# Normalized tokens stored from ScalarE's queue, and a reordered opening, in a linear-attention and mixture-of-experts kernel

## The chip, the cores and the metric

The kernel runs on one core of a Trainium2 chip. The metric is device time in microseconds (us) of one execution, lower is better. The core has five engines with a queue each: TensorE (PE, matrix products into PSUM), VectorE (DVE), ScalarE (ACT), GpSimd (POOL), and SyncE (SP), which issues transfers. ScalarE and GpSimd issue transfers too. [...]

## The reference

The input is 4 batches of 1,024 tokens of 256 channels, so 4,096 tokens. All is float32.

```
xn = layernorm(x)                       # no scale, no offset, eps 1e-5
y  = x + attention(xn) + ffn(xn)
attention: q, k, v = xn @ w_q.T, ...    # 16 heads of 16 channels, elu(.)+1 on q and k
           local  = causal linear attention, state carried from chunk to chunk of 128 tokens
           memory = the same queries read against 4 stored memories, coarse and fine, mixed by a gate
           output = (g * memory + (1-g) * local) @ w_o.T
ffn:       logits = xn @ gate_weight.T; the two best of 8 experts for each token
           each expert and one shared expert: silu(xn @ wg.T) * (xn @ wu.T) @ wd.T
```

What matters for the change is the first line: each token's 256 channels get a mean and a variance, and the normalized token feeds everything else.

## The kernel before, in words

**Tiling.** Tokens are taken in 8 blocks of 512, each held as 4 tiles of 128 tokens (partitions) by 256 channels. Block `b` lives in one SBUF tile called `x_b`. That tile serves twice: first it holds the input tokens, normalized in place, and then the same bytes are overwritten by the values `v` of the block (line 367, with small fills from GpSimd on lines 372 and 373). So the values of a block can be written only when every reader of its normalized tokens has finished.

**Readers of a normalized block.** There are two. TensorE transposes it (line 344), and a transfer stores it to the DRAM tensor `xns` (line 335), from which the expert stage later gathers rows by index (line 990).

**The opening stage.** It has four steps for each block, and the string `ahead` (line 1185) gives their order over blocks by hand:

- `S`, `statistics`: on VectorE, a `bn_stats` and a `bn_aggr` for each of the 4 tiles (lines 303, 304), then, once for block 0, once for each pair of blocks 1 and 2, 3 and 4, 5 and 6, and once for block 7, an add on VectorE and a power on GpSimd that makes `rstd` (lines 309, 312).
- `N`, `normalize`: `shift` on VectorE (319), tiles 2 and 3 on VectorE (326), tiles 0 and 1 on ScalarE (331), then the store to `xns` on SP's queue (335).
- `T`, `transpose_x`: for each of two pairs of tiles, four transposes on TensorE (344) and one copy to `xnT` on ScalarE (347).
- `V`, `values`: for each pair, the product with `w_vg` on TensorE (362), then ScalarE copies `v` into `x_b` (367) and the expert logits into `lgs` (371), and GpSimd fills the gaps (372, 373). Its PSUM pool `ps_v` has two buffers, one for each pair in flight.

The other words of `ahead` are small set-up steps: `masks` and `memories` on VectorE, `gates` on VectorE and ScalarE, `living` on TensorE and VectorE, and `route` on VectorE, which picks experts for the first half of the tokens.

**Transfers ahead of it.** SP's queue carries the 8 loads of `x` (512 KB each), then the memories and small vectors, then `w_o` and the shared expert's weights (lines 121 to 144), then the 8 stores to `xns`, then 8 copies of 512 KB from `x` to the DRAM tensor `sums` (line 1209, DRAM to DRAM, needed when the experts add their results), and two fills from a zero tile (1210, 1211). ScalarE's queue carries `w_vg`, `w_q` and `w_k`.

**After the opening.** Projections of queries and keys, a sort of the tokens by expert, then 32 rounds of attention mixed with 71 expert tiles, and a tail that adds the parts. These follow hand-weighted lists that the change leaves alone.

Of the kernel before, what the change touches and what calls it, by code (L numbers as in the profile page):

```python
# [11 lines left out]
ALU = mybir.AluOpType  # L12
AX = mybir.AxisListType

P = 128
NT = 4
TB = P * NT
EPS = 1e-6
LN_EPS = 1e-5
# [3 lines left out]
def linear_attention_moe_kernel(  # L23
# [28 lines left out]
    nc = tc.nc  # L52
# [17 lines left out]
    NBLK = T // TB  # L70
# [29 lines left out]
    def load_x(blk):  # L100

        wide = big.tile([P, NT, VW], FP, tag="tok", name=f"x_{blk}")
        xb = wide[:, :, :H]
        nc.sync.dma_start(
            xb, x[blk * TB : (blk + 1) * TB, :].rearrange("(n p) h -> p n h", p=P)
        )
        st["x", blk] = xb
        st["wide", blk] = wide

    for blk in range(NBLK):  # L110
        load_x(blk)

    def load_weight(w, name, engine=nc.sync):
        t = const.tile([P, NC, w.shape[1]], FP, tag=name, name=name)
        engine.dma_start(t, w.rearrange("(k p) c -> p k c", p=P))
        return t

    wvg = load_weight(w_vg, "wvg", nc.scalar)
    wq = load_weight(w_q, "wq", nc.scalar)
    wk = load_weight(w_k, "wk", nc.scalar)  # L120
    raw = const.tile([P, NC, NMN, D1], FP, tag="raw", name="raw")
    nc.sync.dma_start(
        raw[:, :, 1:NMN, :], memories.rearrange("(c p) m k -> p c m k", p=P)
# [33 lines left out]
    neghalf = const.tile([P, 2 * NT], FP, tag="neghalf", name="neghalf")  # L157
# [70 lines left out]
    gates = const.tile([P, H], FP, tag="gates", name="gates")  # L228
# [61 lines left out]
        nc.vector.tensor_scalar(alive, tot[:, :NMN], EPS, None, ALU.is_ge)  # L290


    def statistics(blk):

        xb = st["x", blk]
        if blk == 0 or blk % 2:
            st["mv"] = small.tile([P, 2, NT, 2], FP, tag="mv", name=f"mv_{blk}", bufs=3)
            st["rstd"] = small.tile([P, 2, NT], FP, tag="rstd", name=f"rstd_{blk}", bufs=3)
        mv, rstd = st["mv"], st["rstd"]
        at = (blk + 1) % 2 if blk else 0  # L300
        for i in range(NT):
            stats = small.tile([P, 6], FP, tag="stats", name=f"stats_{blk}_{i}")
            nc.vector.bn_stats(stats, xb[:, i, :])
            nc.vector.bn_aggr(mv[:, at, i, :], stats)
        st["norm", blk] = mv[:, at], rstd[:, at]
        if blk % 2 == 0 or blk == NBLK - 1:
            n = at + 1
            some = rstd[:, :n].rearrange("p b i -> p (b i)")
            nc.vector.tensor_scalar(
                some, mv[:, :n, :, 1].rearrange("p b i -> p (b i)"), LN_EPS, None, ALU.add  # L310
            )
            nc.gpsimd.tensor_tensor(some, some, neghalf[:, : n * NT], ALU.pow)

    def normalize(blk):

        xb = st["x", blk]
        mv, rstd = st.pop(("norm", blk))
        shift = small.tile([P, NT], FP, tag="shift", name=f"shift_{blk}")
        nc.vector.scalar_tensor_tensor(
            shift, mv[:, :, 0], -1.0, rstd, ALU.mult, ALU.mult  # L320
        )
        xnT = io.tile([P, NC, TB], FP, tag="xnT", name=f"xnT_{blk}")
        st["xnT", blk] = xnT
        half = NT // 2
        for i in range(half, NT):
            nc.vector.tensor_scalar(
                xb[:, i, :], xb[:, i, :], mv[:, i, 0:1], rstd[:, i : i + 1],
                ALU.subtract, ALU.mult,
            )
        for i in range(half):  # L330
            nc.scalar.activation(
                xb[:, i, :], xb[:, i, :], AF.Identity,
                bias=shift[:, i : i + 1], scale=rstd[:, i : i + 1],
            )
        nc.sync.dma_start(
            xns[blk * TB : (blk + 1) * TB, :].rearrange("(n p) h -> p n h", p=P), xb
        )

# [843 lines left out]
        return runs  # L1182


    ahead = "S0 S1 masks N0 T0 S2 S3 N1 N2 V0 T1 T2 S4 memories V1 S5 N3 N4 V2 T3 T4 S6 gates V3 S7"
    ahead += " N5 N6 V4 living T5 T6 N7 V5 route V6 T7 V7"
    other = {
        "masks": masks, "memories": memories_by_group, "gates": gates_of_heads, "living": living,
        "route": lambda: [None for _ in route(0)],
# [1 line left out]
    with tc.tile_pool(name="ps_v", bufs=2, space=bass.MemoryType.PSUM) as ps_v:  # L1191
        for what in ahead.split():
            if what in other:
                other[what]()
                continue
            blk = int(what[1:])
            if what[0] == "S":
                statistics(blk)
            elif what[0] == "N":
                normalize(blk)  # L1200
            else:
                for pair in range(NT // 2):
                    (transpose_x if what[0] == "T" else values)(blk, pair)
# [3 lines left out]
    for blk in range(NBLK):  # L1207
        rows = slice(blk * TB, (blk + 1) * TB)
# [110 lines left out]
```

## Time and profile before

| what | value |
|---|---|
| median of 3 runs | 736.98 us (736.46 to 739.15) |
| the profiled execution's own time | 731.18 us |
| its span, first to last instruction | 729.5 us |
| busy: PE, DVE, POOL, ACT | 653.1, 455.9, 386.0, 266.8 us |
| PE busy in the first 60.1 us | 40.78 us |
| PE busy from 60 to 90 us | 29.8 us |
| PE busy from 300 to 600 us | 294.5 us |

The span is cut into a start (to 60.1 us, all eight blocks normalized, transposed and projected to values), a dense middle, and a tail. In lines from the timeline the first number is the start in us, the second the time that the group took, then engine, line, operation, output and input, and in brackets the engine's idle time before it with what ended it. A line of the list of waits reads: engine and line that waited, whom it waited for, us in total, number of waits, longest.

### The profile page before, as it was taken

How to read it: one execution, taken by the hardware profiler on the slowest of the kernel's cores; microseconds unless marked ns; L12 is line 12 of the kernel's file. 1: busy time of each engine (PE TensorE's matmuls, PEld its weight loads, DVE VectorE, ACT ScalarE, POOL GpSimd, SP SyncE). 2: the span in 40 equal slices, each digit the busy share in tenths (PEclk: the TensorE clock that was granted, in tenths of full speed). 3: DMA queues.
4: the chain of work that ended last, by engine and by line, in shares of the span. 5: the costliest groups of instructions: out<-in, count | busy, mean ns of one | idle time of the engine just before them, and what ended most of it. 6: DMA issues, size and time to landing. Idle time of an engine off the chain costs nothing. (4 is left out here: it accounts for less than half of the span.)

```text
span 729.5 us, 14268 instructions
## 1 busy us (share of the span) xinstructions
PE 653.1 (90%) x5084; PEld 465.3 (64%) x5084; DVE 455.9 (62%) x1193; ACT 266.8 (37%) x614; POOL 386.0 (53%) x436
## 2 busy tenths in 40 slices
PE   3599986879999999999999999999999998997295
PEld 3485465756676776766676767666776665676274
DVE  6444888984656665665666646656666556667262
ACT  3365443423433443334433443344332433333010
POOL 3210034553656675655566666466664656666464
PEclk9799989999999999999999999999999999999598
DMA  9456000013444564454444544454554545552563
GB/s 292 156 198 190 0 1 1 2 52 89 106 116 99 123 127 96 104 119 106 116 116 107 128 109 120 93 129 101 122 126 96 134 112 108 130 127 40 153 200 123
DMA packets 86563, 81.51 MB, mean 112 GB/s; under 512 B 7629, under 2 KB 84093, under 8 KB 86365
## 3 DMA queue, kind: packets, MB, share of 16 engines
q1 hardware_dynamic: 67629, 57.00, 27.3%
q0 software_dynamic: 13632, 18.62, 15.5%
q10 hardware_dynamic: 5232, 4.99, 2.0%
q8 instruction: 40, 0.66, 0.4%
q14 instruction: 30, 0.25, 0.1%
HBM read 62.62 MB, written 22.15 MB: 116 GB/s over the span
## 5 line engine op out<-in xcount | busy, mean ns | idle before, releaser
L1058 POOL DMA_INDIRECT sums<-y,islot x71 | 113.4, 1597 | 70.6 <-DMA sums<-y,islot 15.1
L1042 DVE SCALAR_TENSOR_TENSOR hidden<-hidden,phe 128x176 f32<-128x176 f32 x71 | 23.8, 335 | 122.4 <-ACT hidden L1041 122.4
L1036 PE MATMUL phe<-wgu,turned 128*128 128x352 f32 x276 | 96.9, 474 | 2.5 <-ACT turned L1029 2.1
L698 DVE TENSOR_TENSOR sT<-quad,causal 128x512 f32<-128x512 f32 x128 | 80.4, 681 | 8.3 <-PE quad L691 7.8
L828 POOL TENSOR_TENSOR cg<-coarse,gates 128x256 f32<-128x256 f32 x32 | 24.3, 760 | 109.3 <-DVE h L883 61.1
L990 POOL DMA_INDIRECT xg<-xns,islot x71 | 70.6, 994 | 17.7 <-issue 9.7
L1049 PE MATMUL pye<-wdn,turned 88*128 88x256 f32 x284 | 75.5, 388 | 4.2 <-PE pu L786 3.0
L1036 PEld LDWEIGHTS phe<-wgu,turned 128*128 128x128 f32 x276 | 48.5, 191 | 26.2 <-issue 6.4
L1049 PEld LDWEIGHTS pye<-wdn,turned 88*128 88x128 f32 x284 | 50.1, 189 | 20.1 <-issue 8.5
L1053 ACT ACTIVATE y<-pye,wslot 128x256 f32<-128x256 f32 x71 | 33.6, 473 | 70.6 <-PE pye L1049 70.3
L846 POOL TENSOR_TENSOR fm<-fm 128x512 f32<-128x512 f32 x32 | 41.7, 1304 | 26.2 <-DVE prob L892 13.1
L1041 ACT ACTIVATE hidden<-phe 128x176 f32<-128x176 f32 x71 | 22.6, 318 | 86.7 <-PE phe L1036 79.7
L1029 ACT COPY turned<-pte 128x512 f32<-128x512 f32 (+1 forms) x71 | 41.2, 580 | 35.6 <-PE pte L1027 34.6
L953 PE MATMUL po<-wd,h 128*128 128x256 f32 (+1 forms) x192 | 49.5, 395 | 0.8 <-ACT oc L868 0.7
L905 PE MATMUL pg<-xnT,wg 128*128 128x512 f32 (+1 forms) x96 | 48.2, 627 | 0.0
L919 PE MATMUL psu<-xnT,wu 128*128 128x512 f32 (+1 forms) x96 | 46.1, 603 | 0.5 <-DVE loc L751 0.5
L835 DVE TENSOR_TENSOR fm<-quad,rw 128x512 f32<-128x512 f32 x64 | 42.2, 680 | 0.0
L953 PEld LDWEIGHTS po<-wd,h 128*128 128x128 f32 (+1 forms) x192 | 35.8, 196 | 7.7 <-ACT oc L868 1.2
L362 PE MATMUL pv<-wvg,xnT 128*128 128x264 f32 x128 | 33.1, 420 | 8.2 <-ACT xnT L347 8.2
L560 POOL TENSOR_TENSOR held<-ones,two 128x213 f32<-128x213 f32 (+1 forms) x22 | 16.0, 737 | 44.5 <-DVE ones L540 44.5
L806 PE MATMUL quad<-mem,sqT 32*128 32x170 f32 x512 | 27.6, 328 | 9.1 <-DVE sT L698 9.1
L894 DVE SCALAR_TENSOR_TENSOR o<-diff,prob,loc 128x256 f32<-128x256 f32 x32 | 33.1, 1035 | 3.4
(210 smaller groups left out, 1374.5 us busy)
## 6 DMA issues: line engine op xcount, KB each, us to landing
wgu<-in_w_gate_dram SPq DMA_DIRECT2D x71, 176.0 KB
wgu<-in_w_up_dram SPq DMA_DIRECT2D x71, 176.0 KB
wdn<-in_w_down_dram SPq DMA_DIRECT2D x71, 176.0 KB
x<-in_x_dram SPq DMA_DIRECT2D x8, 512.0 KB
xns<-x SPq DMA_DIRECT2D x8, 512.0 KB
sums<-in_x_dram SPq DMA_DIRECT2D x8, 512.0 KB
part<-sums SPq DMA_DIRECT2D x12, 256.0 KB
out_dram<-acc ACTq DMA_DIRECT2D x12, 256.0 KB
```

Of the source, the lines that this page charges most:

```text
L698: nc.vector.tensor_mul(sT, quad[:, g, :].rearrange("p (c t) -> p c t", t=P), causal[:, None, :].to_broadcast([P, NC * 2, P]),)
L835: nc.vector.tensor_mul(fm[:, c].rearrange("p g m (r k) -> p g (m r) k", k=HD), quad[:, :, c * KM + KX + KN : (c + 1) * KM].rearrange("p g ...
L846: nc.gpsimd.tensor_add(fm[:, :, 0:2, :], fm[:, :, 0:2, :], fm[:, :, 2:4, :])
L905: nc.tensor.matmul(pg[:n, :], wg[:, k, f * P : f * P + n], xnT[:, k, :], start=(k == 0), stop=(k == NC - 1),)
L919: nc.tensor.matmul(pu[:n, :], wu[:, k, f * P : f * P + n], xnT[:, k, :], start=(k == 0), stop=(k == NC - 1),)
L953: nc.tensor.matmul(po[:, :H], st["h", blk, f][:k, tok], wd[:k, f, :], start=(f == 0), stop=False)
L990: nc.gpsimd.indirect_dma_start(out=xg, out_offset=None, in_=xns, in_offset=bass.IndirectOffsetOnAxis(ap=islot[:, j : j + 1], axis=0),)
L1029: nc.scalar.copy(dst[:, lo:hi], pt[:, lo:hi])
L1036: nc.tensor.matmul(ph[:, : 2 * F], xgT[:, k, :], wgu[:, k].rearrange("p g f -> p (g f)"), start=(k == 0), stop=(k == NC - 1),)
L1049: nc.tensor.matmul(py[:, :H], hT[:FH, f, :], wdn[:, f, :], start=(f == 0), stop=(f == 1))
L1053: nc.scalar.activation(y, py[:, :H], AF.Copy, scale=wslot[:, j : j + 1])
L1058: nc.gpsimd.indirect_dma_start(out=sums, out_offset=bass.IndirectOffsetOnAxis(ap=islot[:, j : j + 1], axis=0), in_=st.pop(("y", j)), in_of ...
```

## The change

There are four edits. The tokens of block 0 are loaded in two parts of 256 KB, the second from ScalarE's queue. `w_q` and `w_k` move from ScalarE's queue to SP's, behind the tokens. The stores to `xns` move from SP's queue to ScalarE's. And `statistics` can do half a block, with a new order of the steps: block 1's statistics come in two halves around the normalization of block 0, and each block's transposes (`T`) come just before its own values, with the statistics, normalizations and set-up steps placed differently among them.

```diff
-        nc.sync.dma_start(
-            xb, x[blk * TB : (blk + 1) * TB, :].rearrange("(n p) h -> p n h", p=P)
-        )
+        parts = 2 if blk == 0 else 1
+        n = NT // parts
+        for part in range(parts):
+            rows = slice((blk * NT + part * n) * P, (blk * NT + (part + 1) * n) * P)
+            (nc.scalar if part else nc.sync).dma_start(
+                xb[:, part * n : (part + 1) * n],
+                x[rows, :].rearrange("(n p) h -> p n h", p=P),
+            )
...
     wvg = load_weight(w_vg, "wvg", nc.scalar)
-    wq = load_weight(w_q, "wq", nc.scalar)
-    wk = load_weight(w_k, "wk", nc.scalar)
+    wq = load_weight(w_q, "wq")
+    wk = load_weight(w_k, "wk")
...
-    def statistics(blk):
+    def statistics(blk, some=slice(0, NT)):
...
-        if blk == 0 or blk % 2:
+        if some.start == 0 and (blk == 0 or blk % 2):
...
-        for i in range(NT):
+        for i in range(some.start, some.stop):
...
-        if blk % 2 == 0 or blk == NBLK - 1:
+        if some.stop == NT and (blk % 2 == 0 or blk == NBLK - 1):
...
-        nc.sync.dma_start(
+        nc.scalar.dma_start(
             xns[blk * TB : (blk + 1) * TB, :].rearrange("(n p) h -> p n h", p=P), xb
         )
...
-    ahead = "S0 S1 masks N0 T0 S2 S3 N1 N2 V0 T1 T2 S4 memories V1 S5 N3 N4 V2 T3 T4 S6 gates V3 S7"
-    ahead += " N5 N6 V4 living T5 T6 N7 V5 route V6 T7 V7"
+    ahead = "S0 S1a N0 S1b S2 T0 N1 N2 V0 S3 masks T1 S4 V1 T2 N3 N4 memories V2 S5 T3 S6 gates V3 N5"
+    ahead += " N6 T4 S7 V4 N7 T5 living V5 T6 route V6 T7 V7"
...
-            blk = int(what[1:])
+            blk = int(what[1])
             if what[0] == "S":
-                statistics(blk)
+                half = {"a": slice(0, NT // 2), "b": slice(NT // 2, NT)}
+                statistics(blk, half[what[2]] if what[2:] else slice(0, NT))
```

## The prediction, written before the result was known

> **What bounds the kernel now.** I read the 40 slices first: PE is dense from slice 4 on, so an edit of the opening pays only by the time at which the opening hands over. Then the timeline of PE, ACT and POOL for the first 62 us. TensorE's row:
>
> ```profile
> 11.15 2.03 PE L344 MATMUL pt<-ident,x 128*128 128x128 f32 x8 [11.15 <-ACT x L331]
> 13.01 4.92 PE L362 MATMUL pv<-wvg,xnT 128*128 128x264 f32 x16
> 17.77 1.91 PE L344 MATMUL pt<-ident,x 128*128 128x128 f32 x16
> 27.48 9.77 PE L362 MATMUL pv<-wvg,xnT 128*128 128x264 f32 x32 [7.81 <-ACT xnT L347]
> 38.83 7.29 PE L362 MATMUL pv<-wvg,xnT 128*128 128x264 f32 x32
> ```
>
> Idle to 11.15, idle from 19.68 to 27.48, and then the same two blocks of values cost 9.77 us where the next two cost 7.29. From 27.48 TensorE has practically no gap until the queries start (60.29; values end near 60.25), and it is busy 29.8 of the 30 us after that. So what shifts the end of the last values shifts everything. The causes, from the list of waits and the timeline:
>
> ```profile
> ACT x L367 <- DMA xns<-x: 8.0, 1, 8.0
> POOL x L372 <- DMA xns<-x: 15.0, 4, 10.6
> 19.17 31.24 SPq L335 DMA_DIRECT2D xns<-x  x8
> 25.71 0.59 ACT L367 COPY x<-pv 128x512 f32<-128x512 f32 x1 [7.97 <-DMA xns<-x]
> 26.00 1.64 POOL L312 TENSOR_TENSOR rstd<-rstd,neghalf 128x8 f32<-128x8 f32 x1
> 10.31 0.15 DVE L319 SCALAR_TENSOR_TENSOR shift<-mv,rstd 128x4 f32<-128x4 f32 x1
> ```
>
> V0's copies overwrite block 0, so they wait for its store. SP issues that store only at 19.17, behind all weights, and it lands at 25.7. Behind the blocked copies on ACT stand T1's and T2's copies, hence PE's 7.81. POOL's `rstd` of blocks 3 and 4 waits behind the blocked fills.
>
> [...] While tokens (1,024 B packets, SP's q1) and `w_vg` (1,056 B, ACT's q10) were both queued, 3.5 to 4.5 us:
>
> ```profile
> q1 hardware_dynamic: 202, 0.21, 57.8%
> q10 hardware_dynamic: 175, 0.18, 50.3%
> ```
>
> That is near one packet each, in turn. While the copies to `sums` ran, 56 to 60 us:
>
> ```profile
> DMA packets 70, 1.15 MB, mean 287 GB/s; under 512 B 35, under 2 KB 35, under 8 KB 35
> ```
>
> 35 packets are tiny; the other 35 moved 1.15 MB, about 32 KB each. The copies' packets are 32 times as large as those of an `xns` store. [...]
>
> [...] (columns: stretch, length, PE busy, clock, DMA share, GB/s); PE stopped at 19.68:
>
> ```profile
> 21.00:22.00 1.00, 0.00 (x0) 1.00 1.02 360
> 22.00:23.00 1.00, 0.00 (x0) 0.54 1.09 367
> 31.00:32.00 1.00, 1.00 (x3) 0.50 0.00 0
> ```
>
> A gap of 2.9 us lost the clock, and it returned only at 32.2, 4.7 us after PE resumed: 9.77 - 7.29 = 2.5 us lost.
>
> **The change part by part**, on the clock of the profiled execution. It took 731.18 us (span 729.5, 1.7 around it), 5.8 below the median of the runs shown; I add the difference to that median.
>
> *First load in two.* Block 0 shared the engines with 264 KB of `w_vg`; now its two halves share only with each other. 264 KB at 366 GB/s is 0.74 us: S0 starts at 4.6 instead of 5.36. Bounds: 0 to 1 us.
>
> *Half of S1 and no masks ahead of N0.* `rstd` was ready at 8.93 (POOL 7.88 + 1.05) but DVE reached `shift` at 10.31, behind S1 and `masks`. Half of S1 (1.06 us) fits under POOL's 1.05, so 1.38 us go. Together T0 starts at 9.04 (-2.1) and V0's products end at 15.6 instead of 17.75.
>
> *Store 0 from ACT.* ACT ends N0 at 9.5. An issue costs ACT 0.36 to 0.46 (its output stores in the tail); here it is covered by ACT's idle 0.78 us before T0's copy, elsewhere it lies in ACT's row. The tokens and this store share 366 GB/s, so 512 KB take 2.9 us, and 1.2 to land (fastest store seen 2.6, less 1.4 of moving): about 14.3. The wait of 7.97 goes.
>
> *What is late next.* DVE ends S2 at 12.3, POOL's power takes 1.65: N1 can start on ACT at 14.25. N1 and N2 are 1.09 each, two issues 0.4 each with their waits, V0's copies 1.1, T1's first copy 0.6: V1 starts at 19.1 instead of 27.48. PE idles 2.5 us instead of 7.8 and, I take it, keeps its clock (bound: 2.5 us if not).
>
> *The new order costs gaps.* Before, T3 T4 and T5 T6 ran as pairs, so a block's values never waited for a copy. Now each T stands directly before its own V, and ACT must first copy the previous values (0.7), then T's first pair (0.6). Before, this happened once (T7 to V7, 0.37). Worse where a normalization is between on ACT: N5 and N6 (2 x 1.09 + 2 x 0.4 = 3.0) now stand ahead of T4's copies, N7 (1.5) ahead of T5's. Following ACT's row in program order, PE's gaps become: V2 0.35, V3 0.65, V4 3.25, V5 1.75, V6 0.25, V7 0.3: 6.55. Seven V of 3.64, six T of 0.95 and these: 19.1 + 25.5 + 5.7 + 6.55 = 56.85 against 60.25: **a gain of 3.4 us, if all stores land in time**.
>
> *The copies to `sums` come early.* They follow the weights on SP. Before, the `xns` stores stood ahead and held them until 50.46. Now nothing does. SP seems to issue a transfer when the eighth before it has landed:
>
> ```profile
> SPq L115 <- DMA x<-in_x_dram: 2.2, 2, 1.1
> SPq L133 <- DMA x<-in_x_dram: 0.3, 1, 0.3
> ```
>
> (its 14th to 16th issue ended waits for block loads 5 to 7.) With `w_q` and `w_k` in SP's row the weights are issued by 21.6 and moved by 24.0; then 8 copies of 1.65 us each (8 of them took from 52.5 to about 66) keep q1 busy to 37.2. Stores 1 and 2 (issued 15.4 and 17.0) share with small packets and land by 22.4. **Store 3 is issued at 25.6**: in every engine its 32 packets of 1 KB alternate with packets of 32 KB, one in 1.65 us. Seven get through by 37.2; the other 25 take 1.1 us, plus landing: 39.2. V3's copies need it at 31.15. Behind them on ACT stand N5, N6 and T4's copies: 39.2 + 1.1 + 3.0 + 0.6 = 43.9, when V4 can start, instead of 37.15: +6.75. PE idles 10 us there, so its clock falls: +2.5, as above. 56.85 + 9.25 = 66.1: **5.8 us later than before**. Store 4 lands 1.4 later, before V4's copies; stores 5 to 7 come after the copies.
>
> Bounds of this unknown: if a turn took many packets of the store (or shared by bytes), it lands at about 31 and costs 0; at one packet a turn, 9.25. I take the latter, since near-equal packets alternated one for one above.
>
> *The rest at nothing.* `w_q`, `w_k` behind the tokens: needed at 57, landed by 20. `masks`, `memories` and the statistics are hidden as DVE was busy 29.5 of 60.1 us; without that cover some 2 us each. The zero tile's fill, which held ACT for 2.4 us near 65, is now long done; PE idled 0.2 there, so at most 0.2.
>
> Sum: 736.98 + 5.8 = 742.8. As the PE is dense from 60 to 90, nothing later absorbs it.
>
> **The rivals.**
> *A: the stores are not starved* (several packets a turn, or a share by bytes). For it: [...] total bandwidth suffices. Against it: the one-for-one packets. Then -3.4, or -0.9 if V4's 3.25 us gap costs the clock: 733.6 to 736.1. This ends on the other side. It decides by when store 3 lands: V4 starts 4.7 later, so with the clock lost the kernel is level at a landing of 33.3, without at 35.8.
> *B: partly starved*, about 8 packets a turn: four turns, lands at 33.8, V4 at 38.5, +1.35, and 1.5 of clock: 736.4.
> *C: a larger gain*. My gaps of 6.55 rest on ACT's strict order and could be half: 732. ACT's fills are short, and the old V7 gap was only 0.37; but the trace shows ACT in program order everywhere.
> *D: the copies start before store 2 has landed.* Margin 1.6 us. V2 waits too, V3 starts near 40 instead of 29.3: 748.
>
> **How the numbers follow.** Mine 0.56 (740 to 746 by itself: the copies may end 2 us sooner or later, the clock cost 1 to 2.5); A 0.22, B 0.08, C 0.08, D 0.06. Half a per cent, 3.7 us, is what a measurement tells from no change. Faster by that: nearly all of C and a fifth of A, 0.12. Slower: 0.85 of mine and D, 0.54. Within: 0.34. The range 733.5 to 746.5 leaves out most of C and the best of A (0.13) and the top of mine and D (0.06).
>
> **What would show it.** Right: V1's products near 19, no wait of V0 for its store; SP's copies to `sums` issued from about 22; ACT waiting some 8 us for `xns` ahead of V3's copies; a PE gap of about 10 us near 34 to 44 and half clock after it; queries starting near 66. Wrong: V3's copies near 31 with no wait, V4 starting near 37, queries starting near 57; or V1 later than 21, if the clock is lost in its gap.

## The result, and the profile after

The changed kernel is slower. Its median is 745.72 us (743.82 to 750.05, 4 runs) beside 736.72 us (735.52 to 739.15, 4 runs) for the kernel before on the same chip. The ratio is 1.0144, with a 95% interval of 1.0108 to 1.0181. The direction was forecast, the amount was not: +5.8 us was forecast, and +9.0 (difference of the medians) to +10.6 (ratio) was measured. The profiled execution took 746.38 us (span 744.5).

TensorE's row in the timeline of the changed kernel (start, time of the group, and in brackets the idle time before it with what ended it), to set beside the row of the kernel before:

```profile
9.12 2.04 PE L350 MATMUL pt<-ident,x 128*128 128x128 f32 x8 [9.12 <-ACT x L337]
21.57 6.75 PE L368 MATMUL pv<-wvg,xnT 128*128 128x264 f32 x16 [4.48 <-ACT xnT L353]
29.57 3.83 PE L368 MATMUL pv<-wvg,xnT 128*128 128x264 f32 x16 [0.37 <-ACT xnT L353]
38.06 5.36 PE L368 MATMUL pv<-wvg,xnT 128*128 128x264 f32 x16 [3.79 <-ACT xnT L353]
48.33 5.34 PE L368 MATMUL pv<-wvg,xnT 128*128 128x264 f32 x16 [4.04 <-ACT xnT L353]
56.43 3.83 PE L368 MATMUL pv<-wvg,xnT 128*128 128x264 f32 x16 [1.54 <-ACT xnT L353]
...
70.23 5.31 PE L606 MATMUL pq<-xnT,wq 128*128 128x512 f32 x12
```

The long values rows are V1, V2, V3, V4 and V5. The first transposes start 2.03 us earlier (9.12 for 11.15) and V1 starts 5.9 earlier than the pair V1 V2 did (21.57 for 27.48). From there all is lost again: the queries start at 70.23 for 60.29, 9.94 us late. After the queries' start this execution ran 674.3 us to the end of its span and the one of the kernel before 669.2. In a second pair of profiles (below, at the end of the experiments) that part took 671.1 and 672.4, the other way about. So, as far as two pairs of profiles show, the opening's 10 us are the change, and the rest varies between executions.

Three gaps of 3.8 to 4.5 us stand ahead of V1, V3 and V4, and each of those three costs 5.3 to 6.8 us where an undisturbed one costs 3.83. The granted clock says why. The stretches of 1 us (columns: stretch, length, PE busy, clock, DMA share, GB/s) before and in V1:

```profile
20.00:21.00 1.00, 0.00 (x0) 0.85 0.04 11
26.00:27.00 1.00, 1.00 (x3) 0.50 1.08 383
```

PE stopped at 17.1; in the slice from 20 the clock falls, and in the slice from 26, 4.4 us after PE has resumed, it is still at half.

In finer slices of this trace the clock changes at 20.71, 27.54, 37.77, 41.19, 48.02 and 51.43 us, each a whole multiple of 3.41 us from the next. In the profile of the kernel before it changes at 22.09 and 32.31, three times 3.41 us apart. By calculation, 3.41 us at half clock do 1.7 us less of work than at full clock, and V3 and V4, with one such stretch each from 37.77 and from 48.02, took 5.36 and 5.34 for 3.83. V1 took 6.75 us in this profile and 5.94 in a second one of the same kernel.

What ACT waited for is in the list of waits of the changed kernel (engine, line, whom it waited for, us in total, number, longest):

```profile
POOL x L378 <- DMA xns<-x: 15.3, 3, 11.0
ACT x L373 <- DMA xns<-x: 4.5, 1, 4.5
ACT x L337 <- DMA sums<-in_x_dram: 3.4, 1, 3.4
ACT x L337 <- DMA wk<-in_w_k_dram: 2.7, 1, 2.7
```

The second row is the starved store of the forecast. The last two are new and were not forecast. A normalization on ACT (L337) neither reads nor overwrites `w_k` or `sums`. ACT's timeline shows what in truth waited, and SP's shows the copies:

```profile
17.74 0.37 ACTq L341 DMA_DIRECT2D xns<-x  x1
18.22 1.09 ACT L337 ACTIVATE x<-x,shift,rstd 128x256 f32<-128x256 f32 x2 [2.69 <-DMA wk<-in_w_k_dram]
...
33.99 0.37 ACTq L341 DMA_DIRECT2D xns<-x  x1
34.41 1.09 ACT L337 ACTIVATE x<-x,shift,rstd 128x256 f32<-128x256 f32 x2 [3.42 <-DMA sums<-in_x_dram]
...
43.15 0.59 ACT L373 COPY x<-pv 128x512 f32<-128x512 f32 x1 [4.55 <-DMA xns<-x]
```

```profile
23.70 6.89 SPq L1216 DMA_DIRECT2D sums<-in_x_dram  x8
```

Block 1 was normalized by 15.5, but its store was issued only at 17.74. Block 3 was normalized by 31.0, and its store went out at 33.99. VectorE's part of both was done earlier, by 15.1 and 23.2. The issue itself takes 0.37 us. In between ACT stood still, and everything behind it in ACT's row stood too. The idle time is booked on the next computing instruction, which is why the list of waits names L337.

Once issued, store 3 still did not move. DMA queues of the changed kernel (queue, packets, MB, share of the 16 engines; q1 is SP's, q10 ACT's), first for 34 to 36 us, then for 38 to 40 us:

```profile
q1 hardware_dynamic: 36, 0.59, 91.5%
...
q1 hardware_dynamic: 119, 0.38, 57.2%
q10 hardware_dynamic: 113, 0.12, 16.3%
```

Between 34 and 36 us there is no packet of ACT's queue at all, while the copies to `sums` move theirs of 32 KB. The store's first packets come between 38 and 39, 4.3 us after its issue.

### The profile page after: what moved, and what is told of

It reads as the page before. It is cut to its first block, busy times and chain, and to the rows that moved or that the text cites. A ratio compares the mean times of both kernels' runs of the same rounds, so it can differ in the third digit from the quotient of the medians.

```text
span 744.5 us, 14262 instructions
## 1 busy us (share of the span) xinstructions
PE 662.8 (89%) x5084; PEld 472.5 (63%) x5084; DVE 454.2 (61%) x1193; ACT 266.6 (36%) x614; POOL 386.2 (52%) x436
## 5 line engine op out<-in xcount | busy, mean ns | idle before, releaser
L1035 ACT COPY turned<-pte 128x512 f32<-128x512 f32 (+1 forms) x71 | 41.1, 579 | 38.3 <-PE pte L1033 32.6
L959 PE MATMUL po<-wd,h 128*128 128x256 f32 (+1 forms) x192 | 51.3, 406 | 0.8 <-ACT oc L874 0.7
L368 PE MATMUL pv<-wvg,xnT 128*128 128x264 f32 x128 | 38.0, 461 | 14.9 <-ACT xnT L353 14.9
L368 PEld LDWEIGHTS pv<-wvg,xnT 128*128 128x128 f32 x128 | 28.8, 232 | 22.5 <-ACT xnT L353 16.7
```

Source lines behind the costliest of these rows:

```text
L368: nc.tensor.matmul(pv[:, j, : H + E], xnT[:, k, i * P : (i + 1) * P], wvg[:, k, :], start=(k == 0), stop=(k == NC - 1),)
L959: nc.tensor.matmul(po[:, :H], st["h", blk, f][:k, tok], wd[:k, f, :], start=(f == 0), stop=False)
L1035: nc.scalar.copy(dst[:, lo:hi], pt[:, lo:hi])
```

## The experiments

The theory after this reading has three parts. (1) The copies to `sums`, issued early at 23.7, hold up the stores of blocks 3 and 4. (2) The new order of the steps costs time by itself. (3) Moving the stores removes V0's wait and is a gain by itself. The rivals were that the order alone is to blame, or the move of the stores alone, or that the packets' size (32 KB against 1 KB) starves the stores, as I had forecast. The start of the queries, given for each run below, is the end of the opening. Each kernel's median was compared with that of the kernel before on the same chip; that one was 731.60, 735.15 and 734.46 us on the three chips used here.

### 1. Hold the copies back

The change, with only the last block's store left on SP. The copies stand behind it there, so they cannot be issued before block 7 is normalized.

```diff
-        nc.scalar.dma_start(
+        (nc.sync if blk == NBLK - 1 else nc.scalar).dma_start(
             xns[blk * TB : (blk + 1) * TB, :].rearrange("(n p) h -> p n h", p=P), xb
```

> The changed kernel with one more edit: the store of block 7's normalized tokens goes back to SP's queue, so the copies to sums stand behind it and cannot be issued before about 47 us. Theory 1 (the copies, issued early, hold store 3 and with it ScalarE): ScalarE's wait for xns ahead of V3's copies goes, V3's products start near 34 instead of 38.1, V4's near 42 instead of 48.3, the queries start at 61 to 63 instead of 70.2, ratio to the kernel before 1.000 to 1.005. Theory 2 (the new order of the steps costs the time, whatever the transfers do): queries start at 68 to 70, ratio 1.012 to 1.016.

Measured: 735.03 us, ratio 1.0048 (1.0027 to 1.007). TensorE's row, with V3, V4 and the queries, then SP's copies:

```profile
33.52 3.83 PE L368 MATMUL pv<-wvg,xnT 128*128 128x264 f32 x16 [0.51 <-ACT xnT L353]
...
42.00 5.51 PE L368 MATMUL pv<-wvg,xnT 128*128 128x264 f32 x16 [3.78 <-ACT xnT L353]
...
63.52 5.31 PE L606 MATMUL pq<-xnT,wq 128*128 128x512 f32 x12
```

```profile
49.64 5.19 SPq L1216 DMA_DIRECT2D sums<-in_x_dram  x8
```

V3 no longer waits, ACT waits neither for `sums` nor for `xns`, and the queries start 6.7 us earlier than in the changed kernel (63.52 for 70.23). So holding the copies is worth 6.7 us of the opening between these two profiles. 1.2 of it is V1's shorter stretch at half clock (5.52 for 6.75), which the copies can't have caused: in the changed kernel they are issued at 23.70, after V1's start, and in experiment 8, where they are issued from 31.35, V1 took 6.73. The kernel is still slower than before, and V4's gap of 3.78 us is there without any store in its way. Part 1 holds, and it is not all.

### 2. The stores alone

The kernel before, with one word changed.

```diff
-        nc.sync.dma_start(
+        nc.scalar.dma_start(
             xns[blk * TB : (blk + 1) * TB, :].rearrange("(n p) h -> p n h", p=P), xb
```

> The kernel before with one edit: the stores of the normalized tokens go to ScalarE's queue; the order, the loads and the weights stay. Theory 1: V0's wait for its store goes (V1's products near 21 instead of 27.5), but the copies to sums start at about 20 and catch store 3, so V3's copies wait to about 36 to 40 and V4's products start then; queries start at 55 to 60, ratio 0.993 to 1.000. Theory 2: the whole removed wait is gained, with the clock, since the old order is kept: queries start near 51 to 53, ratio 0.988 to 0.990.

Measured: 733.93 us, ratio 1.0035 (1.0022 to 1.0049); the queries start at 62.23. V0's wait is gone and V1 starts at 21.91 for 27.48, but the copies, released at 22.33, take it back:

```profile
34.12 1.09 ACT L331 ACTIVATE x<-x,shift,rstd 128x256 f32<-128x256 f32 x2 [5.02 <-DMA sums<-in_x_dram]
43.52 0.59 ACT L367 COPY x<-pv 128x512 f32<-128x512 f32 x1 [4.53 <-DMA xns<-x]
```

The queries came later than either expectation had them (55 to 60 at the most). The move of the stores is a loss of its own in this form, by what it releases behind them.

### 3. All of the change but the order

The change, with the order string of the kernel before.

```diff
-    ahead = "S0 S1a N0 S1b S2 T0 N1 N2 V0 S3 masks T1 S4 V1 T2 N3 N4 memories V2 S5 T3 S6 gates V3 N5"
-    ahead += " N6 T4 S7 V4 N7 T5 living V5 T6 route V6 T7 V7"
+    ahead = "S0 S1 masks N0 T0 S2 S3 N1 N2 V0 T1 T2 S4 memories V1 S5 N3 N4 V2 T3 T4 S6 gates V3 S7"
+    ahead += " N5 N6 V4 living T5 T6 N7 V5 route V6 T7 V7"
```

> The changed kernel with the order of the steps of the kernel before (whole statistics, paired transposes); loads, weights and stores as changed. Theory 1: store 3 is still caught by the copies and V3's copies wait to about 40, but V3's and V4's transposes are done by then and normalization of 5 and 6 does not stand before them, so only part is lost: queries start at 58 to 62, ratio 0.998 to 1.004. Theory 2: the loss is in the order, so it goes wholly: queries start near 52 to 55, ratio 0.988 to 0.992.

Measured: 734.43 us, ratio 1.0036 (1.0022 to 1.0049); the queries start at 61.73, 8.5 us before those of the changed kernel. The early copies still hold ACT (7.2 us for `sums`, 6.8 of them before the issue of store 3 and 0.4 the issue, and 3.3 for `xns`). So the new order is a loss in the opening too, and with 8.5 us between these profiles a larger one than the early copies (6.7).

### 4. The copies in small packets

The change, with the copies written so that each packet has 1 KB, as a store's has.

```diff
-        nc.sync.dma_start(sums[rows, :], x[rows, :])
+        nc.sync.dma_start(
+            sums[rows, :].rearrange("(n p) h -> p n h", p=P),
+            x[rows, :].rearrange("(n p) h -> p n h", p=P),
+        )
```

> The changed kernel with the copies to sums written so that each packet is one row of 1 KB instead of 32 KB; same bytes, same place in the program. If a turn at an engine is one packet of each queue (the step of the prediction), store 3 now alternates one for one, lands within 4 us of its issue, V3's copies start at 36 to 38 instead of 43.2 and queries start near 63 to 65, ratio 1.004 to 1.007. If what is issued first on either queue goes first whatever the packet size, store 3 still waits until the copies are through: V3's copies near 43, queries near 70, ratio 1.012 to 1.016.

Measured: 738.52 us, ratio 1.0079 (1.0054 to 1.0104); the queries start at 69.06. Store 3 was now issued at 31.28 without a wait, but V3's copies waited for it until 40.60, for 5.0 us. DMA queues from 31 to 34, from 34 to 37, and from 37 to 38 us:

```profile
q1 hardware_dynamic: 996, 0.99, 108.6%
...
q1 hardware_dynamic: 808, 0.81, 80.8%
q10 hardware_dynamic: 273, 0.28, 26.9%
...
q10 hardware_dynamic: 190, 0.19, 54.6%
q1 hardware_dynamic: 195, 0.19, 53.8%
```

From its issue at 31.28 up to 34, for 2.7 us, store 3 has no packet, although the copies' packets are as small as its own. By 37 it has 273. At the 190 of the next microsecond these take 1.4 us, so by this estimate its first came near 35.6, 4.3 us after its issue. From 37 to 38 both queues share, with nearly equal numbers of packets. So the packets' size is not what holds the start of the store. V3's copies at 40.60 lie between the two expectations (36 to 38, and near 43).

What does hold it is not shown. In experiment 1, with SP's queue empty, the first packet of store 3 came 0.9 us after its issue (29.75, then 30.65). With SP's queue in use the delay was 3.9 us for store 0 of the changed kernel, behind tokens and weights, 4.3 for its store 3, behind the copies, and about 4.3 here by the estimate. Whether the order of issue over both queues decides is not shown: SP issued its copies here from 23.84 to 33.74, before and after store 3's issue. Nor is it the engines' bandwidth alone: store 1 of the changed kernel, issued at 17.74, had its first packet just before 21.0, while from 18 to 20.9 us the DMA engines were 10% busy, with 310 packets of under 512 B.

### 5. The stores alone, with the copies held

The kernel before, with the stores of blocks 0 to 6 on ACT and that of block 7 on SP, ahead of the copies.

```diff
-        nc.sync.dma_start(
+        (nc.sync if blk == NBLK - 1 else nc.scalar).dma_start(
             xns[blk * TB : (blk + 1) * TB, :].rearrange("(n p) h -> p n h", p=P), xb
```

> The kernel before with the stores of blocks 0 to 6 from ScalarE's queue and block 7's from SP's, so that the copies to sums stay behind it; order, loads and weights as before. If the early copies were what ate the gain of the stores from ScalarE: no wait for sums or xns beyond 1 us on ScalarE after 25 us, V3's products near 33, queries at 54 to 56 (62.2 with the stores alone), ratio 0.990 to 0.995. If moving the stores is worth nothing by itself: queries near 60 to 62, ratio 1.000 to 1.004.

Measured: 731.33 us, ratio 0.9943 (0.9926 to 0.996): faster than both kernels. TensorE's row, with V1 V2, V3 V4 and the queries:

```profile
22.14 9.08 PE L362 MATMUL pv<-wvg,xnT 128*128 128x264 f32 x32 [1.67 <-ACT xnT L347]
...
33.19 7.39 PE L362 MATMUL pv<-wvg,xnT 128*128 128x264 f32 x32 [0.23 <-ACT xnT L347]
...
55.30 5.31 PE L600 MATMUL pq<-xnT,wq 128*128 128x512 f32 x12
```

ACT has no wait for `sums` or `xns` of a microsecond or more up to the queries, and these start 5.0 us earlier than in the kernel before. So the move of the stores is worth what it was meant to be, if the copies stay behind one of them.

### 6. All of the change but the order, with the copies held

Experiments 1 and 3 together.

```diff
-        nc.scalar.dma_start(
+        (nc.sync if blk == NBLK - 1 else nc.scalar).dma_start(
...
-    ahead = "S0 S1a N0 S1b S2 T0 N1 N2 V0 S3 masks T1 S4 V1 T2 N3 N4 memories V2 S5 T3 S6 gates V3 N5"
-    ahead += " N6 T4 S7 V4 N7 T5 living V5 T6 route V6 T7 V7"
+    ahead = "S0 S1 masks N0 T0 S2 S3 N1 N2 V0 T1 T2 S4 memories V1 S5 N3 N4 V2 T3 T4 S6 gates V3 S7"
+    ahead += " N5 N6 V4 living T5 T6 N7 V5 route V6 T7 V7"
```

> The changed kernel with the order of the steps of the kernel before and block 7's store from SP's queue (so the copies are held). Against the run with the new order and held copies (queries at 63.5, ratio 1.0048) this gives the cost of the order. If the new order costs what its gaps sum up to (6 us and some clock): queries at 53 to 56, ratio 0.988 to 0.995. If the order is neutral: queries near 62 to 63.

Measured: 731.58 us, ratio 0.9943 (0.9921 to 0.9965); the queries start at 54.70. With it the table is whole. Start of the queries, for the kernels that have all of the change's transfers:

| | copies held | copies early | cost of early copies |
|---|---|---|---|
| old order | 54.70 | 61.73 | 7.0 |
| new order | 63.52 | 70.23 (the change) | 6.7 |
| cost of the new order | 8.8 | 8.5 | |

That the two losses add up so nearly is in part luck of the clock. Beside its length in an undisturbed row, V1 took 2.9 us more in the change and 1.7 more in experiment 1, where the slices of both profiles show half clock. V1 and V2 together took 1.7 more in experiment 6, and no more in experiment 3; for these two the clock is inferred from the length of the row. V1 and V2 of experiments 3 and 6, whose order is the same:

```profile
21.26 7.39 PE L368 MATMUL pv<-wvg,xnT 128*128 128x264 f32 x32 [1.79 <-ACT xnT L353]
21.53 9.07 PE L368 MATMUL pv<-wvg,xnT 128*128 128x264 f32 x32 [1.86 <-ACT xnT L353]
```

With V1's clock taken out, the early copies cost 8.7 in the old order and 5.5 in the new one, and the order 8.8 with the copies held and 5.6 with them early: the two overlap by some 3 us. With experiment 5 the whole change can be taken apart in steps: 60.29 before; stores moved, copies held, 55.30 (-5.0); loads in the new way 54.70 (-0.6); new order 63.52 (+8.8); copies early 70.23 (+6.7). The -0.6 of the loads is one profile beside another, and the two ratios, 0.9943 both, don't show it.

Where the order's 8.8 us are can be read off the rows of experiments 1 and 6, which start V1 at the same time, 21.55 and 21.53, and take 1.7 us each more than an undisturbed row at V1. From there the gaps ahead of values sum to 6.4 in the new order (0.37, 0.51, 3.78, 0.99, 0.37, 0.37 for V2 to V7) and to 0.9 in the old (0.17, 0.35, 0.37): 5.5. Six single groups of transposes at 1.04 stand against two pairs and one at 4.9 (T2 was already done in the gap ahead of V1): 1.3. V4 takes 5.51 after its gap for 3.83: 1.7. That is 8.5 of the 8.8.

The length of a gap alone does not sort the slow rows from the others. In experiments 5, 6 and 2 the values V1 and V2 took 9.08, 9.07 and 9.07 us after single gaps of 1.67, 1.86 and 1.34; in experiment 3 they took 7.39 after one of 1.79, and V5 of the change took 3.83 after one of 1.54. The time without products of values sorts these five: from the end of the values before to the start of the next, it was 3.86, 4.19 and 3.87 us in the first three, and 3.54 and 2.76 in the other two. In the profiles of the change and of the kernel before, where the slices give the clock, it fell four times (20.71, 37.77 and 48.02; 22.09), each time with no product in the 3.41 us ahead of it; in the kernel before these held 1.0 us of transposes. This is an observation, and no run here was made to test it.

### 7. A faster start, and the weights last

Experiment 6, with block 1's statistics in halves about N0 as in the change, and SP's weights in another order: `w_q`, `w_k` and the small vectors after `w_o` and the shared expert's. By the theory of the issue's wait, store 1 should then go out at once.

```diff
-    wq = load_weight(w_q, "wq")
-    wk = load_weight(w_k, "wk")
...
+    wq = load_weight(w_q, "wq")
+    wk = load_weight(w_k, "wk")
...
-    ahead = "S0 S1 masks N0 T0 S2 S3 N1 N2 V0 T1 T2 S4 memories V1 S5 N3 N4 V2 T3 T4 S6 gates V3 S7"
+    ahead = "S0 S1a N0 S1b S2 T0 N1 N2 V0 S3 masks T1 T2 S4 memories V1 S5 N3 N4 V2 T3 T4 S6 gates V3 S7"
```

> The run before with two more edits: half of block 1's statistics before and half after block 0's normalization, with block 3's statistics and the masks after V0 (as changed); and the small vectors, then w_q and w_k, loaded last on SP's queue. The issue of store 1 waited to 17.7 for the landing of w_k, the eighth transfer before it counting both queues; now the eighth before it is a load of tokens, so it should be issued by 16.5 and V1's products start by 20. Queries at 51 to 54, ratio 0.983 to 0.991. If the wait was for something else, store 1's issue stays at 17.7 and queries come at 53 to 56.

Measured: 732.38 us, ratio 0.9965 (0.9948 to 0.9981); the queries start at 55.42, later than expected and 0.7 later than in experiment 6. ACT's issues of stores 1 and 2:

```profile
15.32 0.37 ACTq L341 DMA_DIRECT2D xns<-x  x1
...
19.68 0.37 ACTq L341 DMA_DIRECT2D xns<-x  x1
```

Store 1 goes out as soon as N1 is done (14.20 + 1.09). But then store 2's issue waits: N2 is done at 16.9, the issue is at 19.68. V1 starts at 21.91 all the same. The wait was moved by one store, not removed. That an issue stood until an earlier transfer had landed is shown by the waits of the changed kernel (2.7 us for `w_k`, 3.4 for `sums`), and that with another order on the other queue the wait stood elsewhere is shown by this run (2.2 us ahead of store 1 there, 2.8 ahead of store 2 here). The profile names no transfer for the wait here, so which one is waited for is not shown. By time of issue `w_k` is the seventh transfer before store 1 in the changed kernel, not the eighth. Whether the wait is the chip's own or a semaphore wait in the built program is not shown either.

### 8. Store 3 on SP

The change, with store 3 on SP ahead of the copies, and all others on ACT.

```diff
-        nc.scalar.dma_start(
+        (nc.sync if blk == 3 else nc.scalar).dma_start(
             xns[blk * TB : (blk + 1) * TB, :].rearrange("(n p) h -> p n h", p=P), xb
```

> The changed kernel with block 3's store alone back on SP's queue: it is issued near 30, ahead of the copies to sums, which follow it at once; store 4 from ScalarE's queue is issued near 31.3, after two of the copies and before the other six. V3's copies no longer wait. If transfers start in the order of issue over both queues and then share packet by packet, store 4 starts when two copies are through, near 35, and then gets one packet of 1 KB for each of 32 KB in an engine, so it lands only with the last copy, near 44 to 46; if they share by bytes, it lands near 38 to 40. Either way queries at 63 to 66, ratio 1.004 to 1.009.

Measured: 741.47 us, ratio 1.0089 (1.0059 to 1.0118); the queries start at 68.79, later than expected (63 to 66). V3 starts at 34.56 after a gap of 0.37. The price moves on to a later store: store 5's issue stood until 42.92 for a landing of a copy, 2.9 us after its block was normalized, and V4 started at 45.59 after a gap of 6.33. This says that a later store issued while the copies run can pay in its turn, and no more. Store 4 was issued at 31.91, 0.6 us after the first copy (31.35), and the waits of ACT up to V4's copies name no wait for it. How 1 KB and 32 KB packets share is not shown by this.

### 9 and 10. Both kernels again

Nothing is edited; this asks whether the 10 us of the opening and the 5 us after it repeat.

> The changed kernel once more, on the same chip as the kernel before. In the first profiles the changed kernel took 5.1 us longer than the one before after the start of the queries too (674.3 against 669.2). If that is the change's, it comes again: near 674, ratio 1.013 to 1.018. If it is a matter of the single execution, it is 668 to 672 here, with the opening again near 70, ratio 1.010 to 1.015.

> The kernel before, once more, for a second profile: queries at 60 to 60.6; from there to the end 669 again if this stretch is steady, 669 to 676 if it varies from one execution to the next.

Measured: 745.49 us (743.67 to 746.62) for the change, ratio 1.0154 (1.0118 to 1.019). The kernel before took 734.54 us in its profiled execution, and has a median of 734.46. The queries start at 70.66 and 60.31, 10.35 us apart; from there to the end of the span 671.1 and 672.4 us. So the opening repeats to a few tenths and explains the loss; the 5 us after it in the first pair of profiles don't repeat.

Over all profiles that later part took between 668.3 and 676.9 us, more than a gain of the opening that one wants to see. This leaves a point open: the openings of experiments 5 to 7 end 5.0, 5.6 and 4.9 us earlier than before, and the medians gain 4.2, 4.2 and 2.6 by their ratios; experiments 4 and 8 lose 5.8 and 6.5 where their openings end 8.8 and 8.5 late. What the later stages give and take there was not studied.

## Why the prediction was right in its direction and short in its size

In short, what failed is the part of the sum headed "if all stores land in time". It put the end at 56.85, a gain; experiment 1, where they do land in time, ends at 63.52. It had priced an issue from ACT at 0.4 us without a wait, and had TensorE keep its clock. The copies' term had the right effect, a wrong mechanism and too large a size (9.25 us forecast, 6.7 measured). The two errors have opposite signs. The direction was carried by the copies in the forecast, but with the copies held experiment 1 is still slower than the kernel before (ratio 1.0048), so that the sign was right is partly luck.

**First load, half of S1: right.** T0 was forecast at 9.04 and came at 9.12.

**V0's wait goes: right.** Store 0 landed at about 17 rather than 14.3, yet still before V0's copies came to their turn in ACT's row.

**"An issue costs ACT 0.36 to 0.46": the first step that failed.** The instruction does take 0.37, but here ACT stood before it until an earlier transfer had landed. I had read this wait off SP's row ("SP seems to issue a transfer when the eighth before it has landed") and had not asked whether such a wait holds for ACT too. Here it did, and the landings waited for were of SP's transfers (`w_k` and `sums` in the list of waits). It cost 2.2 us ahead of store 1 and 3.0 ahead of store 3. In experiment 3 the issue moved to ACT held it for 6.8 us.

**"PE idles 2.5 us and keeps its clock": failed by that.** V1 came at 21.57, not 19.1. The gap was 4.48 us, and V1 took 6.75 instead of 3.64. I had named this as what would make the forecast wrong ("or V1 later than 21, if the clock is lost in its gap"). That a gap of 2.5 us would leave the clock alone was my assumption, and nothing in the trace of the kernel before showed it. Here the gaps of 3.79, 4.04 and 4.48 cost the clock, and V5, after one of 1.54, ran at 3.83; but after gaps of 1.34, 1.67 and 1.86 beside transposes V1 and V2 took 9.07, 9.08 and 9.07 (experiments 2, 5 and 6), 1.7 more than the 7.39 of experiment 3. The "gap of 2.9 us" that I read off the trace of the kernel before was misread as well: the gap was 7.81 us long, and its slice from 22 (0.54) puts the fall at 22.1, 2.4 us after TensorE stopped.

**The new order's gaps: right in place and size, without the clock's price.** The forecast end with all stores in time was 56.85. Experiment 1 is that case, and its queries start at 63.52. By the steps from one V's start to the next, the 6.67 us are: V1 late by 2.45; V1 to V2 6.75 for 4.94, +1.81, V1's half clock; V3 to V4 8.48 for 7.84, +0.64; V4 to V5 7.72 for 6.34, +1.38, V4's slow row (5.51 for 3.83) less a smaller gap; all others together +0.39. So 4.3 of the 6.7 lie at V1 and 2.0 at V4. The six gaps themselves were forecast well: 6.55 in sum, and 6.39 in experiment 1. The gap of 3.25 us was forecast for V4 in its cause as well (N5 and N6 ahead of T4's copies on ACT), and 3.78 was measured. But I charged it no clock: the clock's 2.5 us stood in the sum only with the starved store. By the prediction's own rows the order was priced at 7.5 us (37.75 from V1's start to the end, for 30.3 before at full clock); 8.8 was measured, and V4's clock (1.7) more than covers the difference. With V1 late and slow on top, the sum had a gain of 3.4 us where experiment 1 shows a loss of 3.2 against before.

**The copies come early: right, and the step carried the direction.** They were issued from 23.7 (forecast: from about 22).

**"In every engine its 32 packets of 1 KB alternate with packets of 32 KB": failed as a cause.** Store 3 was late, and V3's copies waited for it, as forecast; but in experiment 4, with small packets, its start was held as long (about 4.3 us, by the estimate there, for 4.3) and V3's copies waited 5.0 us. In the changed kernel its packets came only when the copies were nearly through, so they hardly met packets of 32 KB. What holds the start is open. One packet for one was my estimate from the counts of the early tokens and `w_vg` (202 and 175 in a microsecond); both were issued at 0.81, so they could not show how a later store would start.

**The size of that term.** I forecast 9.25 us, all at V4. The copies cost 6.7 (7.0 in the old order), and most of it in two places: V3 comes 8.49 after V2 (5.22 in experiment 1), by the blocked issue, and V4 comes 10.27 after V3 (8.48), by the starved store; of the other 1.6, 1.2 lie between V1 and V2, where the copies can't be the cause (experiment 1), and 0.4 between V4 and V5. So the term was too large by 2.6 and the part without starved stores too small by 6.7: together 4.1, which is 70.23 less the forecast 66.1. The error of the sum is thus mostly in what ACT's blocked issue (2.2 ahead of store 1) and the lost clock (1.8 at V1, and V4's) do, and not in the order's gaps.

**The rivals.** A and B (stores not or partly starved) fell with the late store 3; C, smaller gaps, fell with experiment 1; D had its condition and not its effect: the copies were issued from 23.70, while store 2's packets ran from 23.7 to 27.7, but the copies' own packets began only at 27.2, and V2 started after a gap of 0.37. The forecast that nothing later absorbs the loss held: +9.9 in the opening, +9.0 to +10.6 in the whole.

## What to carry to other kernels

When a transfer leaves a queue, look at what stood behind it there: the store was also the gate that held 4 MB of copies, and one word that kept the last store on the old queue turned a loss of 0.35% into a gain of 0.57%. Charge a transfer issued from a computing engine with a possible wait of that engine for an earlier landing, also one of the other queue (2.2 to 6.8 us here), and with a late start while another queue is in use (3.3 to 4.3 us here, against 0.9 with that queue empty). Where an engine's row follows the order of the program, as ACT's did here, let producers run in pairs ahead of their consumers (queries at 54.70 for 63.52 here), and charge gaps in TensorE's row with the clock as well as with their own length: here gaps of 1.34 to 1.86 us with transposes beside them were followed by values 1.7 us longer in three cases of four.

## What the runs showed of the hardware that I had not expected

- A transfer issued on ACT waited for the landing of an earlier one, also one of SP's queue, and ACT did nothing meanwhile: 2.2 and 3.0 us in the changed kernel, up to 6.8 (experiment 3). Which earlier one it is stays open.
- While SP's queue was in use, the first packet of a store on ACT's queue came late: store 0, issued at 9.59, at 13.5; store 1, issued at 17.74, at 21.0; store 3, issued at 33.99 behind copies, at 38.3. With SP's queue empty it took 0.9 us. Where both were moving 1 KB packets, they moved nearly equal numbers (190 and 195 in one microsecond). Why the start is held is open.
- The eight changes of the granted clock between the first products and the queries, six in the changed kernel and two in the one before, lay whole multiples of 3.41 us apart in each profile. All four falls came after 3.41 us or more without products, one of them although transposes filled 1.0 us of that time.
